# Attention's softmax: the scaling on ScalarE, the fill of the score tiles on VectorE

## The chip, the cores and the metric

The kernel runs on one core of a Trainium2 chip. The metric is the device time of one execution in microseconds (us), here the median of three runs. A core has five engines that run their own instruction streams in order and meet at semaphores: TensorE (PE in the profile, and PEld for its weight loads), VectorE (DVE), ScalarE (ACT), GpSimd (POOL) and SyncE (SP), which here issues DMAs.

## The reference

A block of four layers over x of 8 x 256 x 1024 numbers and a context of the same shape: an autocorrelation, a feed-forward layer with low-rank parts, a masked attention with rotary positions, and a second feed-forward layer. Each is added to x with a gate. The change lies in the attention, which is this:

```python
q = (query @ wq).reshape(bs, s, N_Q_HEADS, D_K).transpose(0, 2, 1, 3)
...
q = _rope(q)
k = _rope(k)
scale = jnp.sqrt(jnp.float32(D_K))
qg = q.reshape(bs, N_KV_HEADS, g, s, D_K)
scores = jnp.einsum('bhgqd,bhkd->bhgqk', qg, k) / scale
masked = jnp.where(mask[:, None, None].astype(bool), scores, -1000000000.0)
w = jax.nn.softmax(masked, axis=-1)
out = jnp.einsum('bhgqk,bhkd->bhgqd', w, v)
out = out.reshape(bs, N_Q_HEADS, s, D_V).transpose(0, 2, 1, 3).reshape(bs, s, N_Q_HEADS * D_V)
return out @ wo
```

There are 32 query heads of 128 in 8 groups that share keys and values. Everything is float32.

## The kernel before, in words

The batch is worked on in two passes of four sequences. In each pass the layers follow one another, so there are two attention stages: one from about 530 to 1620 us and one from about 2190 to 3300 us of the profile. The products with the weights are formed from seven part products each instead of eight (a scheme like Strassen's); that is why a query product has seven matmul groups and several additions on VectorE.

The attention is written as a loop of 16 steps for a pass: two blocks of two sequences, and for each block the eight groups of heads. A step has four visits, one for each sequence and half of the head group. A visit does three things:

- `scores` forms two score tiles of 128 x 512 (name `ps_s`, line 1131) in PSUM and the softmax of each. A tile `s` in SBUF is filled with -1e9 (line 1139), then the scores are copied over it where the mask allows (L1140, copy_predicated). VectorE takes the negative row maxima (L1142). ScalarE takes the exponentials of the two halves and, with each, the row sums (L1145). VectorE inverts the sums (L1152) and multiplies each half of the tile by them (L1154).
- parts of other work are drawn from generators, so that TensorE is never without matmuls: `queries` (L975, the query products of the following step, with their evacuations at L228 to L244 and the rotation at L714 to L717) and the output products of the step before (`outputs`, L1004, in pass one; `outputs_of_two`, L1067, in pass two). Their PSUM tiles share one tag "mm" with four buffers. In pass one GpSimd also makes finer output weights (`finer_weights`, L921 to L924) for pass two, in the second block of sequences.
- `values` takes up the two tiles of the visit before: TensorE transposes them (name `pt`, L1166), ScalarE copies the transposes to SBUF (`wT`, L1172), and TensorE multiplies them with the values (`av`, L1177). ScalarE copies the result (L1185).

There are four `s` buffers, two for each visit, so a tile is free again when the transposes of the visit after have read it. Tiles, semaphores and the order of the instructions on each engine are made by a scheduler from the program order and the dependencies; the order in the profile isn't quite that of the source. In the profile the exponentials of both tiles are often done before the first multiplication, for instance.

After the attention of a pass the second feed-forward layer starts; its first norm (L348, L355) and transposes (L365) are already within the end of the attention. Elsewhere in the kernel, the autocorrelation has a small softmax of its own whose weights are scaled by ScalarE (L587).

Of the kernel before, what the change touches and what calls it, by code (L numbers as in the profile page):

```python
# [14 lines left out]
AF = mybir.ActivationFunctionType  # L15
ALU = mybir.AluOpType
# [26 lines left out]
MASKED = -1.0e9  # L43
# [3 lines left out]
def flamingo_kernel(ctx: ExitStack, tc: tile.TileContext, a: dict, out: bass.AP):  # L47
    nc = tc.nc
# [801 lines left out]
    def attention(p, xt, gq, go, keep, norms, xops, ahead):  # L850
        with (
# [112 lines left out]
            def half(tag, bufs):  # L964
                return w2.tile([P, 2, S], F32, tag=tag, name=tag, bufs=bufs)
# [157 lines left out]
            def scores(step, l, n, qT):  # L1123

                b = step[0] * 2 + n
                kT = kv[step][0]
                got = []
                for i in range(2):
                    ps = ps_sc.tile([P, 2, S], F32, tag="sc", name="ps_s")
                    for t in range(2):  # L1130
                        nc.tensor.matmul(  # L1131
                            ps[:, t, :],
                            qT[i, n][:, l, t * P : (t + 1) * P],
                            kT[:, n * S : (n + 1) * S],
                            start=True,
                            stop=True,
                        )
                    s = half("s", 4)
                    nc.gpsimd.memset(s, MASKED)  # L1139
                    nc.vector.copy_predicated(s, keep[b], ps)  # L1140
                    nmx = stats.tile([P, 2], F32, tag="nmx", name="nmx", bufs=4)
                    nc.vector.tensor_reduce(nmx, s, AX.X, ALU.max, negate=True)  # L1142
                    tot = stats.tile([P, 2], F32, tag="tot", name="tot", bufs=4)
                    for t in range(2):
                        nc.scalar.activation(  # L1145
                            s[:, t, :],
                            s[:, t, :],
                            AF.Exp,
                            bias=nmx[:, t : t + 1],
                            accum_out=tot[:, t : t + 1],  # L1150
                        )
                    nc.vector.reciprocal(tot, tot)  # L1152
                    for t in range(2):
                        nc.vector.tensor_scalar(  # L1154
                            s[:, t, :], s[:, t, :], tot[:, t : t + 1], None, ALU.mult
                        )
                    got.append(s)
                return got
# [67 lines left out]
            for k, step in enumerate(steps):  # L1226
# [9 lines left out]
                for i, (n, l) in enumerate(((0, 0), (0, 1), (1, 0), (1, 1))):  # L1236
                    got = scores(step, l, n, qT)
                    nq = q_fill.get(k, (3, 3, 1, 0))[i]
                    no = o_fill[k][i]
                    fill_from(q_gen, nq)  # L1240
                    mid = min(no, middle)
                    if i > 0:
                        fill_from(o_gen, no - mid)
                    if before is not None:
                        values(*before, lambda: fill_from(o_gen, mid))
                    before = step, l, n, got, oT
                    if i == 0:
                        if len(last) == 1 + paired:
                            o_gen = start_outputs()
                            fill_from(o_gen, no)  # L1250
                        else:
                            fill_from(o_gen, no - mid)
                    if i == 2 and k + 2 < len(steps):
                        if steps[k + 2][1] == 0:
                            blk = steps[k + 2][0]
                            xb = xt[blk * NBT : (blk + 1) * NBT]
                            xops[blk] = query_operands(xb, norms[blk], new_xl, ps_wa, "wa")
                        load_wq(steps[k + 2])
                    if i == 0 and not paired:
                        load_wo(step)  # L1260
                    if i == 0 and p == 0 and step[0] > 0 and step[1] % 2:
                        fine = finer_weights(step)
                    fill_from(fine, 1)
# [308 lines left out]
```

## Time and profile before

| | |
|---|---|
| median of 3 runs | 3361.8 us (3356.34 to 3363.13) |
| the profiled execution | 3351.35 us, its span 3349.6 us |
| granted TensorE clock in it | 0.992 |
| L1154 multiplications (DVE) | 512, mean 560 ns |
| L1139 fills (POOL) | 256, mean 528 ns |
| L1145 exponentials (ACT) | 512, mean 500 ns, and 187 ns each for reading the sums |
| L1172 copies of the transposes (ACT) | 256, mean 588 ns |
| L1140 predicated copies (DVE) | 256, mean 728 ns |

How to read the rows: a group of instructions is named by its line, engine, operation and "out<-in" by the names of the tiles, with the shape (partitions x elements) and the count. Behind the bar stand the busy time in us, the mean of one in ns, and the time that the engine stood idle just before such instructions, with what ended most of it. In a list in order of time the columns are start, duration, engine, line, operation; brackets give the idle time before and its releaser. In a list of waits they are who waited, for whom, the total in us, the number of times and the longest. Busy times of an engine are the time in which at least one instruction ran, so overlapping instructions aren't counted twice. A matmul of 128x256 stands for half of a float32 product: each is issued in two.

ScalarE's busy time in the attention stages is 289 us of 1090 in the first and 302 us of 1110 in the second; VectorE's is 799 and 798, GpSimd's 536 and 560.

### The profile page before, as it was taken

To read this page: it belongs to the slowest core of one execution; us is meant where nothing else is said; L and a number is where in the kernel's file an instruction comes from. 1 tells how busy PE (TensorE), PEld (TensorE's weight loads), DVE (VectorE), ACT (ScalarE), POOL (GpSimd) and SP (SyncE) were. 2 spreads that over 40 slices of the span, in tenths; PEclk is the share of its full clock that TensorE was granted. 3 is DMA by queue.
4 is the path that set the end of the run, shared out by engine and by line. 5 is a ranking of instruction groups with operands and counts; after the bars stand their busy time and mean duration, and the time that the engine had idled before them with its cause. 6 is when DMAs were issued, how large, how long until landed. Compare 5 with 4: busy or idle time off the path is not lost. (4 is left out here: it accounts for less than half of the span.)

```text
span 3349.6 us, 39704 instructions
## 1 busy us (share of the span) xinstructions
PE 3268.8 (98%) x13456; PEld 2408.0 (72%) x13456; DVE 2356.0 (70%) x4561; ACT 844.1 (25%) x2043; POOL 1513.2 (45%) x1437
## 2 busy tenths in 40 slices
PE   8999899999999999999999999999999999999999
PEld 6677456777777766775456677568888888888874
DVE  7787657877777776776647686457776777777773
ACT  1332111322232322222113332113222223222310
POOL 4554112334433475576344442113464554554672
PEclk9999999999999999999999999999999999999999
DMA  7534615333333454554353435043555455555551
GB/s 280 174 113 125 240 59 189 127 136 132 139 126 129 132 207 147 178 190 160 116 189 127 141 120 166 7 159 101 166 182 161 157 168 175 164 168 172 176 186 51
DMA packets 215784, 505.58 MB, mean 151 GB/s; under 512 B 25076, under 2 KB 102900, under 8 KB 215582
## 3 DMA queue, kind: packets, MB, share of 16 engines
q1 hardware_dynamic: 214430, 498.84, 44.2%
q0 software_dynamic: 1152, 4.19, 0.3%
q8 instruction: 108, 1.77, 0.2%
q14 instruction: 94, 0.77, 0.1%
HBM read 394.96 MB, written 108.00 MB: 150 GB/s over the span
## 5 line engine op out<-in xcount | busy, mean ns | idle before, releaser
L717 POOL TENSOR_TENSOR qT<-qT,rope 128x512 f32<-128x512 f32 x128 | 169.3, 1322 | 671.0 <-DVE qT L716 670.9
L975 PE MATMUL ps_q<-xn,wq 128*128 128x256 f32 x1920 | 428.9, 379 | 0.0
L975 PEld LDWEIGHTS ps_q<-xn,wq 128*128 128x128 f32 x1920 | 364.8, 190 | 50.5 <-PE po L677 0.5
L1140 DVE COPY_PREDICATED s<-keep,ps_s 128x512 f32<-128x512 uint8 x256 | 185.5, 728 | 217.9 <-PE ps_s L1131 181.0
L1145 ACT ACTIVATE s<-s,nmx 128x256 f32<-128x256 f32 x512 | 255.9, 500 | 282.7 <-DVE nmx L1142 281.6
L975 PE MATMUL ps_q<-xn_t,wq 128*128 128x256 f32 x1280 | 285.6, 379 | 0.0
L1154 DVE TENSOR_SCALAR s<-s,tot 128x256 f32<-128x256 f32 x512 | 266.1, 560 | 7.5
L1172 ACT COPY wT<-pt 128x512 f32<-128x512 f32 x256 | 138.2, 588 | 526.8 <-PE pt L1166 526.3
L975 PEld LDWEIGHTS ps_q<-xn_t,wq 128*128 128x128 f32 x1280 | 243.2, 190 | 33.1
L370 DVE SCALAR_TENSOR_TENSOR x<-po,tg,x 128x512 f32<-128x512 f32 x248 | 176.4, 743 | 128.0 <-PE po L1319 45.7
L1177 PE MATMUL av<-wT,v 128*128 128x256 f32 x1024 | 246.0, 382 | 1.7 <-ACT wT L1172 1.4
L1131 PE MATMUL ps_s<-kT,qT 128*128 128x256 f32 x1024 | 247.5, 379 | 0.0
L1177 PEld LDWEIGHTS av<-wT,v 128*128 128x128 f32 x1024 | 191.6, 190 | 55.9 <-issue 21.5
L1067 PE MATMUL po<-wo,oI 128*128 128x256 f32 x896 | 215.7, 381 | 1.9 <-issue 1.2
L1131 PEld LDWEIGHTS ps_s<-kT,qT 128*128 128x128 f32 x1024 | 191.8, 190 | 25.5 <-issue 0.7
L1004 PE MATMUL po<-wo,oT 128*128 128x512 f32 x448 | 201.9, 593 | 0.0
L1139 POOL MEMSET s<- 128x512 f32 x256 | 128.7, 528 | 131.9 <-PE pt L1166 124.4
L1067 PEld LDWEIGHTS po<-wo,oI 128*128 128x128 f32 x896 | 169.8, 191 | 25.6 <-issue 1.8
L1142 DVE TENSOR_REDUCE nmx<-s 128x2 f32<-128x512 f32 x256 | 174.4, 684 | 7.7
L1067 PE MATMUL po<-wo,oT 128*128 128x256 f32 x672 | 171.7, 382 | 6.4 <-PE pt L1166 4.0
L253 POOL TENSOR_TENSOR x<-x,part 128x512 f32<-128x512 f32 x48 | 63.4, 1320 | 233.4 <-ACT part L252 233.4
L1185 ACT COPY oT<-av 128x512 f32<-128x512 f32 x128 | 75.0, 586 | 370.1 <-PE av L1177 370.1
(290 smaller groups left out, 6361.4 us busy)
## 6 DMA issues: line engine op xcount, KB each, us to landing
wo<-wo_d SPq DMA_DIRECT2D x144, 512.0 KB, 4.8
wq<-in_wq_dram SPq DMA_DIRECT2D x104, 512.0 KB, 3.5
wq<-wq_d SPq DMA_DIRECT2D x96, 512.0 KB, 3.3
wo<-in_wo_dram SPq DMA_DIRECT2D x56, 512.0 KB, 3.4
wo_d<-fine_t SPq DMA_DIRECT2D x56, 512.0 KB, 3.4
wo<-wo_d SPq DMA_DIRECT2D x96, 256.0 KB, 3.4
w<-w_d SPq DMA_DIRECT2D x36, 512.0 KB, 5.4
wo<-in_wo_dram SPq DMA_DIRECT2D x72, 256.0 KB, 3.3
```

Of the source, the lines that this page charges most:

```text
L370: nc.vector.scalar_tensor_tensor(xs, ps, g, xs, ALU.mult, ALU.add)
L717: nc.gpsimd.tensor_add(dst, dst, t)
L975: nc.tensor.matmul(ps[:, l, :], wops[r][:, l, c, :], xo[r][:, c, :], start=(c == 0), stop=(c == KH - 1),)
L1004: nc.tensor.matmul(po, ops[r][:, h, t * P : (t + 1) * P], wops[r][:, h, :], start=(h == 0), stop=(h == 1),)
L1067: nc.tensor.matmul(po, left[r2][:, h, :], w[:, h, :], start=(h == 0), stop=(h == 1))
L1131: nc.tensor.matmul(ps[:, t, :], qT[i, n][:, l, t * P : (t + 1) * P], kT[:, n * S : (n + 1) * S], start=True, stop=True,)
L1140: nc.vector.copy_predicated(s, keep[b], ps)
L1142: nc.vector.tensor_reduce(nmx, s, AX.X, ALU.max, negate=True)
L1145: nc.scalar.activation(s[:, t, :], s[:, t, :], AF.Exp, bias=nmx[:, t : t + 1], accum_out=tot[:, t : t + 1],)
L1154: nc.vector.tensor_scalar(s[:, t, :], s[:, t, :], tot[:, t : t + 1], None, ALU.mult)
L1172: nc.scalar.copy(wT[i], pt)
L1177: nc.tensor.matmul(av[:, i, :], kv[step][1][:, n * 2 + c, :], wT[i][:, c, :], start=(c == 0), stop=(c == 1),)
```

## The change

The fill of the score tile moves from GpSimd to VectorE, and the multiplication by the inverted sums moves from VectorE to ScalarE, where it is an activation with the function Copy and a scale for each partition. It is done in place, as before. Nothing else is edited; the order of the instructions is made anew by the scheduler.

```diff
                     s = half("s", 4)
-                    nc.gpsimd.memset(s, MASKED)
+                    nc.vector.memset(s, MASKED)
                     nc.vector.copy_predicated(s, keep[b], ps)
...
                     nc.vector.reciprocal(tot, tot)
                     for t in range(2):
-                        nc.vector.tensor_scalar(
-                            s[:, t, :], s[:, t, :], tot[:, t : t + 1], None, ALU.mult
+                        nc.scalar.activation(
+                            s[:, t, :], s[:, t, :], AF.Copy, scale=tot[:, t : t + 1]
                         )
                     got.append(s)
```

## The prediction

> **What bounds the kernel now.** I read the page's engine line first, then its costliest groups, then busy time by stretch, then TensorE's waits inside attention, and last the instructions around the longest of them. All times are microseconds (us) unless marked ns.
>
> ```profile
> PE 3268.8 (98%) x13456; PEld 2408.0 (72%) x13456; DVE 2356.0 (70%) x4561; ACT 844.1 (25%) x2043; POOL 1513.2 (45%) x1437
> ...
> L1154 DVE TENSOR_SCALAR s<-s,tot 128x256 f32<-128x256 f32 x512 | 266.1, 560 | 7.5
> ...
> L1139 POOL MEMSET s<- 128x512 f32 x256 | 128.7, 528 | 131.9 <-PE pt L1166 124.4 <-PE po L668 7.3
> ```
>
> TensorE is the bound. The stretches that hold the two attention stages say so more sharply: it is busy 1075.45 of the 1090 us from 530 to 1620, and 1100.60 of the 1110 from 2190 to 3300. The chain of waits gives TensorE 41% of the span and no other engine more than 1%. So an engine that gets less or more work moves the end only where TensorE waits for it now, or will. Those waits are few. Stage one, then stage two (total, times, longest):
>
> ```profile
> PE pt L1166 <- DVE s L1154: 4.4, 2, 4.2
> PE pt L365 <- DVE xn L355: 3.7, 1, 3.7
> PE po L1004 <- DVE x L370: 2.8, 1, 2.8
> PE po L1004 <- DVE qT L716: 1.4, 2, 0.8
> PE av L1177 <- ACT wT L1172: 1.4, 3, 0.9
> PE po L1004 <- POOL oS L211: 0.6, 1, 0.6
> ```
> ```profile
> PE po L1067 <- PE pt L1166: 4.0, 12, 0.3
> PE po L1067 <- DVE co L1082: 2.0, 1, 2.0
> ```
>
> With three small ones of stage two (1.2, 0.8 and 0.8) and 0.4 more they add up to 23.5 us, 0.7% of the span: no gain in attention can be larger. The instructions around the two longest show where they come from:
>
> ```profile
> 1456.80 8.12 DVE L1154 TENSOR_SCALAR s<-s,tot 128x256 f32<-128x256 f32 x2
> ...
> 1466.35 1.98 PE L1004 MATMUL po<-wo,oS 128*128 128x512 f32 x4 [2.81 <-DVE x L370]
> ...
> 1567.03 8.28 DVE L1154 TENSOR_SCALAR s<-s,tot 128x256 f32<-128x256 f32 x2
> ...
> 1575.19 1.94 PE L1166 MATMUL pt<-ident,s 128*128 128x128 f32 x8 [4.16 <-DVE s L1154]
> ```
>
> Two multiplications of the softmax last 8 us together, and TensorE stands right behind. The release is put down to L370 in the first case, but L370 had only been queued behind L1154.
>
> **The removed multiplications (DVE).** The line's own row gives least, median and longest time in ns:
>
> ```profile
> L1154 DVE TENSOR_SCALAR s<-s,tot x512: 333/353/8016, 579.1 to 3187.5; 128x256 f32<-128x256 f32 x171
> ...
> L587 ACT ACTIVATE w<-w,tot x64: 492/508/511, 84.6 to 2051.6; 128x256 f32<-128x256 f32 x64
> ```
>
> 512 x 560 = 287 us leave DVE. At the median they would be 181; the other 106 are waiting inside the instruction. In each slow one that I looked at, GpSimd was running a tensor operation; in the 8.016 us one at 1567.03, seven of them one after the other (1566.30 to 1574.9). [...]
>
> **The added multiplications (ACT).** L587 is the same operation on the same shape: 512 x 507 ns = 260 us. ACT goes from 844 to about 1104 us, 33% of the span. [...] In the visit that starts at 902.5, the last multiplication ends at 908.4 and the transposes start at 929.2. Four ACT multiplications end at most 2.0 us after the exponentials, so they are hidden by 20 us of other matmuls. If that cover is gone, at the ends of the passes, they show in full.
>
> The new wait is ACT's: each multiplication waits for the reciprocal (L1152), and ACT runs in order. Queued behind it are the copies of the transposed weights (wT, L1172), which the value matmuls (av, L1177) wait for, the copy of the first query product (L228) and of the output products (L1073, L252). L228 comes 0.3 us after the exponentials in nearly every step, but is needed one 3.45 us product later; a delay of 2.0 us is covered. wT is different in the first visits of each pass, where almost nothing lies between transposes and av:
>
> ```profile
> 596.70 1.05 ACT L1172 COPY wT<-pt 128x512 f32<-128x512 f32 x2
> ...
> 597.31 1.99 PE L1177 MATMUL av<-wT,v 128*128 128x256 f32 x8 [0.87 <-ACT wT L1172]
> ```
>
> Here the exponentials end at 596.8. Put 2.03 us of multiplications ahead of the copy, and its first half ends at 599.4 and av starts 2.2 us later than at 597.31. The same reckoning gives 2.2 at 606.41, 1.4 at 2271.84, 1.6 at 2279.75, 1.4 at 2321.74, 0.4 at 588.39 and 0.9 in the last step (3159.63): 10.1 us in all. But six score matmuls (1.46 us) stand behind av in these visits and are ready before it; where TensorE's order takes them first, the five large ones shrink to 0.8, 0.8, 0, 0.1 and 0, and the sum to 3.0. I take **4 us lost**, nearer the covered end because these matmuls wait for nothing that the copy holds.
>
> **The fill, from GpSimd to VectorE.** 256 x 528 ns = 135 us leave POOL. No row has a 128x512 memset on VectorE; those of 128x1 and 128x5 take 59 and 62 ns. From below, the 333 ns that the fastest multiplication needs for half as many elements; from above, the 684 ns of the reduction over the same tile. [...]
>
> Hidden or not: a fill may start when the transposes two pairs back have freed the tile, and is needed by the predicated copy (L1140), mostly 3 to 7 us later. [...] The wait for the transposes now heads VectorE's queue, with evacuations of the "mm" PSUM tiles behind it. [...] What goes is L1140's wait for a GpSimd that is busy making finer output weights (L921 to L924), 34.4 us in 8 waits:
>
> ```profile
> 1222.59 0.73 DVE L1140 COPY_PREDICATED s<-keep,ps_s 128x512 f32<-128x512 uint8 x1 [5.23 <-POOL s L1139]
> ```
>
> **The sum**, against this execution (3351.35 us, span 3349.6):
> - Gone: 4.16 and 2.81 (both L1154); 2.01 at 2643.14, where a 1.73 us multiplication and a second one stand before the L1082 that TensorE waits for; 0.63 and 0.79 at 1245.85 and 1378.6, behind such a wait for the fill (5.23) and slow multiplications (2.81 and 2.41 a pair); 0.33 and 0.26 after 1583 at the end of stage one. Together 11.0.
> - End of stage one: POOL starts L209 at 1592.53 though its input (oT) was there at 1589.53, as finer weights hold it. L209 to L211 and L253 follow, then L370, the norm and L355, for which TensorE waits 3.71 (and 0.64 for L211). Eight fills less in the last four visits are 4.2 us of POOL; up to 3.0 of it can come through, or nothing where the DMAs of the weights pace it. I take 2.
> - Lost: 4 on ACT. The fills cost nothing while the PSUM cover holds.
>
> Net -9 us: this execution would take 3342. The runs' median is 3361.8 (3356.34 to 3363.13), 10 us above the profiled one; I take the change off the median: **3353 us**. What is late next is TensorE itself in the loop, and L355 between the stages. About 0.2%, or 6.7 us, is what a measurement of this kernel can tell from no change, so the forecast lies close to that line.
>
> **Rivals.**
> - *ACT takes it back* (20%): the multiplications go ahead of the wT copies with no cover: 10.1 lost, 11 gained, nothing at the end of the stage: 3361. For it: the exponentials already stand before these copies (the 0.87 us wait). Against: the six matmuls.
> - *The fills stall VectorE* (20%): at the head of an in-order queue they wait for transposes while query and output products fill PSUM. Place: stage two, where TensorE finishes an output product each 0.86 us and VectorE is busy 72%. [...]
> - *The lock stays* (8%): other VectorE work with inputs in SBUF (L355, L211, L1094) stands behind the same rows of GpSimd work in the place of L1154; a third of the gain is left: 3359.
> - *More than the sum* (7%): almost all of the 23.5 us in attention goes except the pass-two tail, with ACT covered: 3340.
>
> **Chances and range.** The forecast has 45%, and its own range is 3346 to 3359 (4 lost becoming 3 or 10; 2 becoming 0 or 3; the medians' spread of 3). Faster by over 0.2% means under 3355: most of the forecast and "more than the sum", 0.45. Within 0.2%: the rest of it, ACT and the lock, 0.30. Slower: the fills and a tail of ACT, 0.25. For 8 in 10: 3340 to 3371.
>
> **What would show it.** Right: no VectorE instruction in attention much over 2 us; no wait of pt or po near 1466 and 1575; L1140 waiting for ps_s alone; ACT near 1104 us and VectorE near 2220; pt to av in the steady loop unchanged. Wrong in step two: L1172 waits behind the multiplications, and av's waits for wT go from 1.4 us to 5 or more. Wrong in step three: a fill above 0.7 us, or waits of TensorE for VectorE all over stage two. The whole is wrong if other VectorE instructions last 8 us beside GpSimd.

## The result, and the profile after

The changed kernel takes **3341.07 us** (median of 4 runs, 3336.68 to 3342.07) beside 3362.47 us of the kernel before (4 runs, 3356.34 to 3364.26). The ratio is 0.9944, with a 95% interval of 0.993 to 0.9958: 21 us, or 0.56%, faster. The profiled execution took 3340.92 us (before 3351.35), its span is 3339.1 us (before 3349.6). So the two profiles show only 10.5 of the 21 us, and where the rest comes from is one of the questions below.

From the page of the changed kernel, the engine line and two groups (busy time and mean of one in ns behind the bar):

```profile
PE 3267.4 (98%) x13456; PEld 2405.0 (72%) x13456; DVE 2221.3 (67%) x4305; ACT 1051.6 (31%) x2555; POOL 1404.9 (42%) x1181
...
L1140 DVE COPY_PREDICATED s<-keep,ps_s 128x512 f32<-128x512 uint8 x256 | 184.8, 727 | 156.0 <-PE ps_s L1131 155.1
...
L1154 ACT ACTIVATE s<-s,tot 128x256 f32<-128x256 f32 x512 | 230.1, 497 | 40.6 <-DVE tot L1152 40.5
```

VectorE lost 134.7 us of work (2356.0 to 2221.3; near 2220 was predicted). The predicated copies no longer wait for GpSimd, and a multiplication on ScalarE takes 497 ns (507 predicted). The line of the fill, with least, median and longest in ns, shows it at 485 ns every time:

```profile
L1139 DVE MEMSET s<- x256: 485/485/485, 546.8 to 3168.1; 128x512 f32 x128
```

TensorE's waits in attention stage one of the changed kernel (total, times, longest):

```profile
PE po L1004 <- POOL oS L211: 6.0, 1, 6.0
PE pt L365 <- DVE xn L355: 1.9, 1, 1.9
PE av L1177 <- ACT wT L1172: 1.6, 1, 1.6
PE po L1004 <- DVE qT L716: 0.9, 5, 0.2
```

The two waits behind L1154 (4.16 and 2.81 us) are gone. In their place, at the very end of the stage, stands a new one of 6 us. Its history, from the changed kernel's list in order of time (start, duration; in brackets the idle time before, and its releaser):

```profile
1582.45 1.28 POOL L922 TENSOR_TENSOR fine_t<-wo,wo 128x512 f32<-128x512 f32 x1 [1.21 <-DMA wo_d<-fine_t]
...
1586.25 1.26 POOL L209 TENSOR_TENSOR oS<-oT 128x512 f32<-128x512 f32 x1
...
1590.12 3.78 PE L1004 MATMUL po<-wo,oS 128*128 128x512 f32 x4 [6.02 <-POOL oS L211]
1595.81 1.94 PE L365 MATMUL pt<-ident,xn 128*128 128x128 f32 x8 [1.91 <-DVE xn L355]
```

GpSimd comes to L209 only when the finer output weights ahead of it in its queue are done, and these wait for the DMAs that store them. The reader should also look at the durations: four matmuls of 128x512 took 3.78 us here. Elsewhere four of the same take 1.88 us. TensorE runs at half its clock after the wait (0.50 was granted, as shown below); that will matter.

The third line of the list, 1.58 us, is ScalarE's: the copy wT stood behind a multiplication that waited for its sum.

```profile
1562.45 0.75 DVE L370 SCALAR_TENSOR_TENSOR x<-po,ntg,x 128x512 f32<-128x512 f32 x1 [1.70 <-POOL x L261]
...
1563.31 0.91 ACT L1154 ACTIVATE s<-s,tot 128x256 f32<-128x256 f32 x2 [4.26 <-DVE tot L1152]
...
1564.73 1.13 PE L1177 MATMUL av<-wT,v 128*128 128x256 f32 x4 [1.58 <-ACT wT L1172]
```

In sum, the idle time between TensorE's matmuls fell from 69.7 to 60.5 us: by 4.0 in stage one, by 5.1 in stage two. Of the latter, 1.7 us is L1082's wait (2.01, now 0.32), and 2.5 us are twelve waits of 0.33 us behind the transposes, now 0.12 us each.

### The profile page after: what moved, and what is told of

Same layout as the page of the kernel before. It is cut to its first block, busy times and chain, and to the rows that moved or that the text cites. A ratio compares the mean times of both kernels' runs of the same rounds, so it can differ in the third digit from the quotient of the medians.

```text
span 3339.1 us, 39371 instructions
## 1 busy us (share of the span) xinstructions
PE 3267.4 (98%) x13456; PEld 2405.0 (72%) x13456; DVE 2221.3 (67%) x4305; ACT 1051.6 (31%) x2555; POOL 1404.9 (42%) x1181
## 5 line engine op out<-in xcount | busy, mean ns | idle before, releaser
L370 DVE SCALAR_TENSOR_TENSOR x<-po,tg,x 128x512 f32<-128x512 f32 x248 | 177.3, 743 | 139.3 <-PE po L1319 44.7
L1154 ACT ACTIVATE s<-s,tot 128x256 f32<-128x256 f32 x512 | 230.1, 497 | 40.6 <-DVE tot L1152 40.5
L1177 PEld LDWEIGHTS av<-wT,v 128*128 128x128 f32 x1024 | 191.4, 190 | 54.8 <-issue 22.2
L1004 PEld LDWEIGHTS po<-wo,oT 128*128 128x128 f32 x448 | 83.0, 191 | 83.2 <-issue 74.8
```

The costliest lines, as they stand in the source:

```text
L370: nc.vector.scalar_tensor_tensor(xs, ps, g, xs, ALU.mult, ALU.add)
L1004: nc.tensor.matmul(po, ops[r][:, h, t * P : (t + 1) * P], wops[r][:, h, :], start=(h == 0), stop=(h == 1),)
L1154: nc.scalar.activation(s[:, t, :], s[:, t, :], AF.Copy, scale=tot[:, t : t + 1])
L1177: nc.tensor.matmul(av[:, i, :], kv[step][1][:, n * 2 + c, :], wT[i][:, c, :], start=(c == 0), stop=(c == 1),)
```

## Experiments

Two theories were to be told apart. Mine: VectorE's multiplication can be held up for as long as GpSimd runs one operation after the other (8.016 us at 1567.03 in the kernel before, beside seven of them); the change gains because the multiplication is no longer held up. The expectations call it the lock theory, and two labels speak of a port; both are names of the author's, and the runs show only how long instructions took. The rivals: the gain comes from the fills, or from VectorE having less to do, or ScalarE gives part of it back. `scale_only`, `fill_only`, `one_port` and `last_left` ran on one chip, `before_nofine`, `after_nofine`, `after_again` and `scale_twice` on a second, the last four on a third; "before" is always the kernel before, run beside them.

### One half of the change at a time

`scale_only` has the multiplication on ScalarE, and leaves the fill on GpSimd:

```
-  nc.vector.tensor_scalar(s[:, t, :], s[:, t, :], tot[:, t : t + 1], None, ALU.mult)
+  nc.scalar.activation(s[:, t, :], s[:, t, :], AF.Copy, scale=tot[:, t : t + 1])
```

> Only the multiplications move to ScalarE; the fills stay on GpSimd. Lock theory (VectorE's multiplications were starved by rows of GpSimd work): the 4.16, 2.81 and 2.01 us waits of TensorE go, the waits of the predicated copy for the fill (34.4 us in 8) stay, so 6 to 9 us of span go, most of the change's 10.5; no VectorE instruction in attention above 2.4 us. Load theory (VectorE simply had too much to do): 287 us leave VectorE instead of the change's net 135, so at least the whole gain of the change or more. If the fill was what mattered, this is no faster than before.

`fill_only` has the fill on VectorE, and leaves the multiplication there:

```
-  nc.gpsimd.memset(s, MASKED)
+  nc.vector.memset(s, MASKED)
```

> Only the fills move to VectorE (256 x 485 ns = 124 us more for it); the multiplications stay on VectorE. Lock theory: the multiplications still last up to some 8 us where GpSimd works without a break, TensorE still waits behind them; only the waits of the copy for the fill go: 0 to 3 us less span. Load theory: VectorE is busier by 124 us, so slower than before by 3 us or more. If the two parts are worth the same, 5 us less.

With before at 3361.08 us (19 runs), `scale_only` took 3337.18 us, ratio 0.9922 (0.9906 to 0.9938). `fill_only` took 3358.01 us, ratio 0.9995 (0.9984 to 1.0005): no difference. The multiplication is the whole of the gain. With the fills alone moved, the long multiplications stay, here the row of L1154 and the wait behind it in stage one of `fill_only`:

```profile
L1154 DVE TENSOR_SCALAR s<-s,tot x512: 227/353/7795, 579.1 to 3195.5; 128x256 f32<-128x256 f32 x171
```
```profile
PE po L1004 <- DVE x L370: 7.3, 3, 2.7
PE po L1004 <- DVE qT L716: 3.9, 6, 0.8
```

The other GpSimd work is enough to hold them up. The second line is a price of the fills: TensorE waits for the rotated queries, 3.9 us in 6 times, where before had 1.4 us in 2.

### The multiplication stays on VectorE, in another form

`one_port` leaves the multiplication and the fill on the engines where they were, and only asks the instruction for a sum along the row as well, which nobody reads:

```
+  one = stats.tile([P, 2], F32, tag="one", name="one", bufs=4)
...
   nc.vector.tensor_scalar(
       s[:, t, :], s[:, t, :], tot[:, t : t + 1],
-      None, ALU.mult
+      0.0, ALU.mult, ALU.add, accum_out=one[:, t : t + 1],
   )
```

> The kernel before, with the multiplication on VectorE in the form that also writes out an accumulator (an unused sum); fills on GpSimd. Same engine and no less work for it: 512 instructions of about 0.43 us with 0.08 us for the accumulator, so 260 us instead of the 181 that the median gave. Lock theory: no multiplication above 0.6 us, TensorE's waits at about 1466, 1575 and 2643 us go, and 5 to 9 us of span with them although VectorE has more to do by instruction count. Load theory: no gain, or slower by a few us.

It took **3333.76 us** (6 runs), ratio 0.9918 (0.9904 to 0.9932), against the same before as the two above. Its row, beside that of L1154 in the kernel before (333/353/8016):

```profile
L1155 DVE TENSOR_SCALAR_CACHE_REDUCE s<-s,tot x512: 458/476/483, 571.2 to 3169.1; 128x256 f32<-128x256 f32 x171
```

The median rose from 353 to 476 ns, and each of the 512 needs another 83 ns to hand over its sum. Yet the longest is 483 ns, and VectorE's busy time falls from 2356.0 to 2313.1 us. That decides what the long multiplications come from: neither less work for VectorE nor ScalarE nor the fill is needed to end them, only a form that wasn't held up in any of its 512 instances.

The whole time is weaker evidence than these durations, for part of it was won elsewhere. In the profile of `one_port` the attention's first query product starts at 534.2 us, in before at 542.2. A VectorE instruction of the autocorrelation (L583), which the edit doesn't touch, takes 7.04 us in before and 1.10 in `one_port`, each beside a row of GpSimd work:

```profile
114.37 7.04 DVE L583 SCALAR_TENSOR_TENSOR w<-took,ex 128x256 f32<-128x256 f32 x1
```
```profile
113.34 1.10 DVE L583 SCALAR_TENSOR_TENSOR w<-took,ex 128x256 f32<-128x256 f32 x1
```

From the first query product of pass two to the end, `one_port` gains nothing (1133.2 us, before 1131.9, the changed kernel 1126.3). What shows the long multiplications is the stretch from the first query product of pass one to the first product of pass two (L796): 1181.7 us in before, 1189.6 in `fill_only`, 1173.0 in `scale_only`, 1174.5 in `one_port`.

### GpSimd's rows taken away

In both kernels the four subtractions that make a finer output weight (L921 to L924) are left out, and the raw weight is stored in their place, with as many bytes. The finer weights are not computed, so these two do less work than the others.

```
-  nc.gpsimd.tensor_sub(t45[:, 1], q[0][1], q[0][0])
...
-  nc.sync.dma_start(wo2_d[g // 2][:, n, 0], t67)
-  nc.sync.dma_start(wo2_d[g // 2][:, n, 1], t45)
+  for k in range(2):
+      flat = w[k].rearrange("p h (j s) -> p h j s", j=2)
+      nc.sync.dma_start(wo2_d[g // 2][:, n, k], flat)
```

> The kernel before, without GpSimd's four subtractions per finer output weight (L921 to L924): the raw weights are stored in their place by as many bytes, so the output is not the reference's. GpSimd's rows in stage one are gone. Theory (a VectorE instruction of one source waits for a whole row of GpSimd operations): the longest L1154 in stage one falls from 8 us to under 3 us, VectorE's idle 18.6 us at the end of stage one goes too, and the time falls by 15 to 25 us. Rival (the long multiplications come from something else, such as a late total): L1154 stays at 7 to 8 us, and only the end of stage one gains, 4 us.

> The changed kernel without the same four subtractions. Theory: the end of stage one (6.02 us for oS and 1.91 us for xn, both behind the finer weights and their stores) goes, so 6 to 9 us below the changed kernel; and since no row of GpSimd is left to wait for in stage one, it is within 8 us of before_nofine, where after and before lie 21 us apart. Rival (the wait at the end comes from the bias load or from the chain of normalisation alone): nothing gained over the changed kernel, as last_left showed, and the distance to before_nofine stays at 15 us or more.

With before at 3360.03 us (9 runs), `before_nofine` took 3332.52 us, ratio 0.9923 (0.991 to 0.9937), and `after_nofine` 3328.83 us, ratio 0.9899 (0.9884 to 0.9915). The distance between the two kernels shrinks from 21 us to 4. The multiplications of `before_nofine` (now line 1146):

```profile
L1146 DVE TENSOR_SCALAR s<-s,tot x512: 328/352/1734, 581.3 to 3164.0; 128x256 f32<-128x256 f32 x171
```

From 8.0 to 1.7 us, about one GpSimd operation (1.3 us): the long ones belong to the long rows. And in `after_nofine` the only wait of TensorE between 1560 and 1622 us is this one, so the 6 us for oS came from the finer weights:

```profile
PE pt L365 <- DVE xn L355: 1.7, 1, 1.7
```

### The end of stage one: another engine for L209 to L212

`last_left` is the changed kernel, but forms the last operands oS on VectorE, so that they need not queue behind the finer weights:

```
+  eng = nc.vector if last[0][0] == steps[-1] else nc.gpsimd
-  got = outputs(last[0][0], left_operands(nc.gpsimd, last[0][1], *s))
+  got = outputs(last[0][0], left_operands(eng, last[0][1], *s))
```

> The changed kernel, with the four additions and subtractions for the last output products of stage one (L209 to L212) on VectorE instead of GpSimd, where they stood behind finer weights for 8.4 us. TensorE's wait of 6.02 us for L211 goes; the wait for L355 (1.91) may grow, as L253 still stands on GpSimd. 3 to 7 us less than the changed kernel. If that wait was only covering another, nothing is gained.

3340.72 us, ratio 0.9942 (0.9926 to 0.9959) to the before of the first group: nothing gained, a miss. The list in order of time shows why:

```profile
1593.44 0.75 DVE L1295 TENSOR_SCALAR bias<-bias,tg 128x1024 f32<-128x1024 f32 x1 [4.08 <-DMA bias<-in_b_dram]
...
1595.72 1.94 PE L365 MATMUL pt<-ident,xn 128*128 128x128 f32 x8 [9.84 <-DVE xn L355]
```

The wait for oS is gone, and the norm that follows is as late as ever: VectorE stands before a scaling of the bias, whose load has not arrived, with the norm's L355 behind it. Two chains end within 1 us of each other here, and taking one away shows the other. L355 starts at 1594.77 us here and at 1594.87 in the changed kernel. Only the two kernels without the subtractions, in which no store waits for one, got rid of most of both: 1.7 us are left in each.

### Does ScalarE give something back?

`after_again` is the changed kernel; `scale_twice` multiplies each tile a second time, by 1.0, in place:

```
   nc.scalar.activation(s[:, t, :], s[:, t, :], AF.Copy, scale=tot[:, t : t + 1])
+  nc.scalar.activation(s[:, t, :], s[:, t, :], AF.Copy, scale=1.0)
```

> The changed kernel once more, beside the other runs of this call, for comparisons without a second chip or day between them. 3336 to 3343 us; the same gaps in TensorE: 6 us at the end of stage one, 1.6 us at the value product before it. Every theory expects the same.

> The changed kernel with every multiplication on ScalarE followed by a second one by 1.0 in place: 512 more at 493 ns, 252 us more of ScalarE, and each half tile ready for its transposes some 0.5 to 1 us later. Theory (ScalarE has cover: the schedule holds the transposes back by more than the multiplication takes): under 8 us lost, at the copies of the transposed scores that queue behind the multiplications. Rival (ScalarE is near the path and takes back what VectorE gives, as priced at 10 us without cover in the prediction): 15 us or more lost, and TensorE waits on L1154 or on L1172 in most visits.

On one chip, `after_again` took 3336.68 us, ratio 0.9934 (0.992 to 0.9947), and `scale_twice` 3336.57 us, ratio 0.9934 (0.9921 to 0.9948). ScalarE's busy time rose from 1051.5 to 1205.6 us and the time did not move. ScalarE has cover for the multiplication and for as much again.

The profile of `after_again` brought something else. It has the same waits in attention as the first (6.2, 1.9 and 1.6 us), but a span of 3327.8 instead of 3339.1 us. Its gaps are only 2.6 us shorter in all: one wait of TensorE in the second Fourier stage (the transforms of the autocorrelation, in pass two) shrank by 4.9 (6.34 us at 1900, now 1.45), because a VectorE instruction (L466) that lasted 6.62 us beside a row of GpSimd work in the first profile took 1.78 us at most in the second, and others grew a little. The rest of the 11.3 us is the clock.

### The clock after a wait

The granted TensorE clock in windows of 4 us (busy time of each engine, then the clock, DMA share and GB/s), for the changed kernel at the wait for oS:

```profile
1584.00:1588.00 4.00, 0.11 (x1) 0.00 (x0) 0.00 (x0) 0.78 (x2) 3.84 (x4) 0.99 0.54 220
1588.00:1592.00 4.00, 1.88 (x3) 0.84 (x4) 0.68 (x1) 0.00 (x0) 4.00 (x4) 0.50 0.97 299
1592.00:1596.00 4.00, 2.09 (x4) 0.55 (x3) 3.86 (x6) 0.00 (x0) 1.74 (x2) 0.50 0.33 136
1596.00:1600.00 4.00, 4.00 (x11) 2.56 (x11) 3.19 (x4) 1.17 (x2) 2.46 (x1) 0.50 0.01 4
1600.00:1604.00 4.00, 4.00 (x9) 1.78 (x8) 2.80 (x3) 0.00 (x0) 1.96 (x2) 0.80 0.40 98
```

TensorE stopped at 1584.11 and started again at 1590.12. The clock fell to 0.50 at 1587.9, after 3.8 us of idleness, and was back at 1601.6, 11.5 us after the restart, with the 1.9 us wait for xn among them. `keep_warm` puts 26 matmuls into the wait, whose product nobody reads:

```
+  late = last[0][1][1][1]
...
+  if not paired:
+      warm = ps_sc.tile([P, 2, S], F32, tag="sc", name="warm")
+      for _ in range(26):
+          nc.tensor.matmul(warm, ident, late, start=True, stop=True)
```

> The changed kernel with 26 more matmuls of 128x512 at the end of stage one, on the last output tile and the identity, whose product nobody reads: some 11 us of TensorE work at 0.43 us each in place of the 6 us wait for oS, so that TensorE does not idle between 1583 and 1595 us. Theory (half the clock is granted for some us after TensorE has idled for 3 us or more, so every such wait is paid about twice): the clock stays 1.0 from 1583 to 1605, the four matmuls of oS take 1.9 us together instead of 3.8, the transposes of xn 1.0 us instead of 1.9, and the clock time lost in stage one falls from 3.4 to 6.8 us to under 1.7; the time gains 0 to 4 us though 11 us of work were added. Rival (the clock falls there for another reason than idleness): the half clock stays, and the added matmuls take 22 us instead of 11, so some 10 us are lost.

My 11 us were mis-sized: each of these float32 products is issued in two, so 52 matmuls at 0.43 us make 22.4 us. The clock did what the theory says:

```profile
1588.00:1592.00 4.00, 4.00 (x10) 1.71 (x9) 0.00 (x0) 0.00 (x0) 3.92 (x4) 1.00 0.94 292
...
1600.00:1604.00 4.00, 4.00 (x10) 1.71 (x9) 0.16 (x1) 0.00 (x0) 0.00 (x0) 1.00 0.00 0
```

It stays at 1.00, and the matmuls of oS take 0.43 us each again. In this run at least, idleness is what brings the half clock. As to time, 3341.99 us stand against 3346.64 of before on its chip, ratio 0.9988 (0.9975 to 1.0002), with 22.4 us of work added. This was another chip than those above, on which before was 14 us faster; the changed kernel itself was not timed there, so what warming gains or costs in time stays open. What this run shows is the clock.

### The kernel before once more

> The kernel before, profiled once more, because its profiled execution (3351) lies 10 us under the median of its runs. Theory (span = 3252 us + TensorE's gaps + the time lost to half clock): at 3360 us the two together come to 106 us where the first profile has 97, through a stalled VectorE instruction in attention or in the Fourier stages or through more windows of half clock. Rival (something else stretches the slower executions): gaps and lost clock stay at 97.

> The same once more, a third profile of the kernel before: the sum 3252 us + gaps + lost clock meets its span within 2 us whatever its time is; the two longest L1154 are again 7 to 8 us, at the same places if the order of work fixes them, elsewhere if they are a matter of chance.

Two more profiles of the unchanged kernel took 3356.65 and 3367.95 us. In both there are **four** multiplications of 8.05 to 8.09 us, near 1195, 1330, 1467 and 1580 us, where the profile that the prediction read had two. One of them, with all that GpSimd did beside it, from the first of these profiles:

```profile
1191.55 8.33 DVE L1154 TENSOR_SCALAR s<-s,tot 128x256 f32<-128x256 f32 x2
```
```profile
1190.77 1.31 POOL L262 TENSOR_TENSOR x<-x,part 128x512 f32<-128x512 f32 x1
1192.00 1.29 POOL L261 TENSOR_TENSOR x<-x,part 128x512 f32<-128x512 f32 x1
1193.22 1.30 POOL L262 TENSOR_TENSOR x<-x,part 128x512 f32<-128x512 f32 x1
1194.44 1.33 POOL L922 TENSOR_TENSOR fine_t<-wo,wo 128x512 f32<-128x512 f32 x1
1195.70 1.30 POOL L923 TENSOR_TENSOR fine_t<-wo,fine_t 128x512 f32<-128x512 f32 x1
1196.93 1.32 POOL L921 TENSOR_TENSOR fine_t<-wo 128x512 f32<-128x512 f32 x1
1198.17 1.30 POOL L924 TENSOR_TENSOR fine_t<-fine_t,wo 128x512 f32<-128x512 f32 x1
```

The multiplication starts in the middle of a row and ends with its last operation, at 1199.5. But a row doesn't always hold it up so long. In the first profile the stalls near 1195 and 1330 us are missing, though the rows are there: multiplications began at 1191.75 and 1324.30 with seven operations of a row still to end, and took 0.62 and 0.60 us; the second of each pair took 1.35. From that profile:

```profile
1324.30 1.87 DVE L1154 TENSOR_SCALAR s<-s,tot 128x256 f32<-128x256 f32 x2
```
```profile
1323.48 1.27 POOL L262 TENSOR_TENSOR x<-x,part 128x512 f32<-128x512 f32 x1
1324.70 1.32 POOL L261 TENSOR_TENSOR x<-x,part 128x512 f32<-128x512 f32 x1
...
1331.08 1.26 POOL L924 TENSOR_TENSOR fine_t<-fine_t,wo 128x512 f32<-128x512 f32 x1
```

Of the multiplications that began with seven operations to end, two of four waited for all of them in the first profile, four of four in each of the others, and two of three in `fill_only`; the rest took less than 0.7 us. What decides isn't known.

TensorE's waits in stage one of `before_p1`, beside 2.8 and 4.4 us in the first:

```profile
PE po L1004 <- DVE x L370: 9.2, 3, 3.1
PE pt L1166 <- DVE s L1154: 4.4, 2, 4.1
```

So the same program has two or four such stalls from one execution to another. For each run the span and the mean granted clock are known, and their product is what its work and gaps take without the half clock. It is 3322.8 us for the profile with two stalls, 3328.1 and 3329.2 for those with four. For the runs of before on the first two chips it averages 3329.5 (19 runs) and 3328.4 (9), for those of the changed kernel 3312.6 (the 4 of the result) and 3312.9 (5). So some 16 of the 21 us are work and gaps, the rest is clock, and the usual run there is like the profiles with four stalls. That it had them is likely but not shown, as those runs have no trace. On the third chip the 15 runs of before average 3322.4, like the profile with two.

### Both remedies on VectorE

`one_port_fill` is `one_port` with the fills on VectorE too.

> [...] Theory (fills cost little where VectorE has slack, and gain little): within 5 us of one_port's 3334, with VectorE 2430 us busy. Rival (the fills on VectorE are what the change owes its gain to, or what stalls it): 8 us or more away from one_port, below or above.

3333.35 us, ratio 0.9963 (0.9949 to 0.9977) to the 3346.64 us of its chip. `one_port` was on another, so the two can't be compared within less than the 14 us between the chips. The traces show why the fills make so little difference. In `one_port`, at the end of stage one, a fill stands behind a finer weight that waits for its store:

```profile
1562.30 1.26 POOL L922 TENSOR_TENSOR fine_t<-wo,wo 128x512 f32<-128x512 f32 x1 [1.13 <-DMA wo_d<-fine_t]
1563.50 0.98 POOL L1139 MEMSET s<- 128x512 f32 x2
1564.05 0.73 DVE L1140 COPY_PREDICATED s<-keep,ps_s 128x512 f32<-128x512 uint8 x1 [5.61 <-POOL s L1139]
...
1568.51 2.08 PE L1184 MATMUL av<-wT,v 128*128 128x256 f32 x4 [5.70 <-ACT wT L1179]
```

In `one_port_fill` that wait is gone, and TensorE waits longer for oS and for the rotated queries instead:

```profile
PE po L1004 <- POOL oS L211: 7.3, 1, 7.3
PE po L1004 <- DVE qT L716: 4.4, 5, 0.9
```

## Why the prediction was right, and where its numbers were wrong

The forecast was 3353 us in a range from 3340 to 3371, and faster; the time is 3341. It is within the range but outside the forecast's own 3346 to 3359. An account of all profiles shows where the missing 12 us lie. "Gaps" is the idle time between TensorE's matmuls, "half clock" the sum of 10 us x (1 - granted clock) over all windows of 10 us; "rest" is the span less both. The last column is the stretch from the first query product of pass one to the first product of pass two, in which the long multiplications lie.

| profile | span | gaps | half clock | rest | stage one |
|---|---|---|---|---|---|
| before, the first | 3349.6 | 69.7 | 27.3 | 3252.6 | 1181.7 |
| before_p1 | 3354.9 | 73.6 | 27.2 | 3254.1 | 1193.0 |
| before_p2 | 3366.2 | 79.4 | 35.9 | 3250.9 | 1195.4 |
| the changed kernel | 3339.1 | 60.5 | 27.2 | 3251.4 | 1175.1 |
| after_again | 3327.8 | 57.9 | 17.2 | 3252.7 | 1172.7 |
| scale_only | 3339.7 | 62.7 | 23.8 | 3253.2 | 1173.0 |
| fill_only | 3355.8 | 76.6 | 22.1 | 3257.1 | 1189.6 |
| one_port | 3329.6 | 62.2 | 15.3 | 3252.1 | 1174.5 |
| one_port_fill | 3336.4 | 61.1 | 20.5 | 3254.8 | 1178.3 |
| last_left | 3338.9 | 63.6 | 25.5 | 3249.8 | 1174.7 |
| scale_twice | 3330.1 | 56.4 | 22.2 | 3251.5 | 1169.3 |
| before_nofine | 3325.6 | 56.2 | 17.0 | 3252.4 | 1162.9 |
| after_nofine | 3327.1 | 55.4 | 18.7 | 3253.0 | 1162.2 |

(`keep_warm`: 3341.0 less 48.5 and 13.6 is 3278.9, and 3256.5 without its 22.4 us of added matmuls.) The rest is the same within 7 us (3249.8 to 3257.1): the span is TensorE's work, its gaps, and its clock. Point by point:

- **TensorE is the bound, and only its waits count: right, but for one thing.** A wait costs its own length, and it can cost some of the clock after it (3.4 us after the 4.16 us wait at 1571.03 in before, nothing after the 2.81 us one at 1463.55). The prediction had no term for the clock. Its limit, "no gain in attention can be larger" than 23.5 us, held for the gaps of one execution; the two later profiles of before have 31.1 and 33.0 us of them there.
- **The multiplications on VectorE: right, though the row was read from one side.** Both stalls went (7.0 us), as did most of the waits of 2.01 (0.32 is left), 0.63 and 0.79 (0.9 in all, in five waits). No VectorE instruction in attention lasts over 2.3 us after the change, so "the lock stays" is out. The longest took 7.8 to 8.1 us in every profile with the plain form and GpSimd's rows, and 0.48 or 1.73 us without the one or the other, so the stalls that were subtracted were real. The row of seven operations that the prediction read at 1567.03 was half of what that trace has: of four multiplications that began with seven operations to end, two (at 1191.75 and 1324.30) took 0.62 and 0.60 us. Both lengths occur, and the prediction had no term for how often.
- **ScalarE: right in kind, 4 us predicted, 1.6 measured,** one wait at 1564.73, where before had 1.4 in three. It isn't at the first visits but near the end of stage one, where the multiplication ahead of the copy waited for a reciprocal that VectorE had queued behind L370, and this for GpSimd. In the first visits the scheduler put copies of wT between the multiplications and score matmuls in front of the value products, so nothing was lost there; `scale_twice` shows that more cover is left. "ACT takes it back" is out. Beside the other form on VectorE it cost nothing: with a mean of 497 ns on ScalarE (`scale_only`) and 476 on VectorE (`one_port`), the stretch that holds stage one took 1173.0 and 1174.5 us.
- **The fills: right that they cost about nothing,** at 485 ns each, 124 us in all. That they cost nothing while the PSUM cover holds, the 2220 us for VectorE and the chance given to a loss by the fills rest on the author's estimates of a fill and of that cover, which no run shows; the runs showed the 485 ns, VectorE busy for 2221.3 us, and in stage one of the changed kernel 0.9 us of TensorE waiting for L716. "The fills stall VectorE" is out. The price shows only where VectorE keeps the multiplications too (3.9 us in `fill_only`, 4.4 in `one_port_fill`).
- **The end of stage one: wrong in sign.** Two us were to be gained; the waits there (0.64 and 3.71, now 6.02 and 1.91) grew by 3.6. The step that failed is "Eight fills less ... are 4.2 us of POOL; up to 3.0 of it can come through". GpSimd did come to L209 6.3 us earlier (1592.53 to 1586.25), but TensorE came to the wait 11.7 us earlier (1595.79 to 1584.11): what it had gained before was partly given back here. The reservation in the same sentence, that the DMAs of the weights pace it, fits the 1.21 us that L922 waits for its store; `after_nofine` shows that the finer weights cause the wait for oS, but takes the subtractions away with the waits, so it doesn't tell one from the other.
- **The twelve waits of 0.33 us in stage two were left out of the sum,** and brought 2.5 us. In `one_port` they are 0.6 us; what sets their length stays open.
- **From the profile to the runs: this is the step that failed most.** "I take the change off the median" carried 9 us, worked out from an execution of 3351 us, over to runs of 3362. In the first profile 7.2 us of waits stood behind L1154 and the L370 after it (2.8 and 4.4), in `before_p1` 13.6 (9.2 and 4.4), and the changed kernel has none of them in either of its profiles. What makes before slower than its profile is, in the two profiles that show it, to a large part the very thing that the change removes. Part of the rest is the clock: with the gaps before and behind it, half clock costs 27 to 36 us in the three profiles of before, 17 and 27 in the two of the changed kernel.

The rival "more than the sum" gave 3340, nearly the time measured. Its mechanism isn't what happened: 10.5 us of gaps are left in stage one and 4.3 in stage two.

## What to carry to other kernels

A VectorE instruction in the middle of a row of GpSimd work can wait until the row ends (8.0 us here, where the median is 0.35); look at the longest of a group, not at its mean, and see what GpSimd ran meanwhile. The remedy needn't be another engine: the form that also writes a sum took 476 ns instead of 353, and 83 for the sum, and none of the 512 was held up (483 ns at most). Before two remedies are called equal by their times, look at what else differs between the profiles: `one_port` gained 8 us ahead of the stage that was edited. And when a stall depends on how two queues happen to meet, one profile is one draw: take a second one before the gain is subtracted from a median.

## What the runs showed of the hardware

- **How long a row of GpSimd work holds up VectorE.** The wait can be for all GpSimd operations that follow each other without a pause, six to seven here (7.2 to 8.1 us), or for the one that runs (0.6 us, in the same place of the same program); which of the two comes isn't known. It isn't only the one-source form: in the Fourier stages a scalar_tensor_tensor with two sources in SBUF lasted 7.09 us (L583 at 114.52) and another 6.62 us (L466 at 1898.18) in the changed kernel, both beside such a row, with TensorE waiting 5.06 and 6.34 us behind them. These are still there to be gained. L583 lasted over 7 us in 12 of the 14 profiles and at most 1.5 us in `one_port` and `one_port_fill` (TensorE idles 5.0 to 5.6 us between 110 and 140 us in those 12, and not at all in these two), L466 over 6.6 us in 7 of the 14 (6.3 to 6.4 us idle between 1870 and 1940); why isn't known. Nor is it known why no tensor_tensor on VectorE, with two sources, lasted over 2.29 us in either kernel.
- **The clock after a wait.** In the clock records of the 14 profiles the granted clock is full or 0.50. A stretch at 0.50 lasts 3.41 us or two to four times that (but for the last, at the end of the profile), and within a profile the stretches start whole multiples of 3.41 us apart. In the two kernels' profiles, 20 falls in all, the 3.41 us ahead of a fall held 1.85 us or more of TensorE's idle time, and none of the other stretches on the same grid, at full clock and within the clock record, more than 1.79; over all 14 profiles it is 1.65 us or more ahead of 122 falls, and 2.00 at most in the 13322 others. A gap's length alone didn't settle what it cost. After a single gap of under 1.9 us the clock lost was nearly always nothing, after gaps of 2.0 to 3.3 us anything from 0 to 3.4 us, after those of 3.6 us and more 1.6 to 6.1 us, each time.
- **Chips.** The kernel before took 3361.1 and 3360.0 us on two chips and 3346.6 on a third. A gain of 21 us on one chip is not known to be 21 on the next.
